# Cross-attention of layer 1: 256 keys of two batches per PSUM bank, the last key apart, and state-space preparation placed between tiles

## The chip, the cores and the metric

The kernel is one program on one core of one Trainium2 chip. The metric is device time in microseconds (us), the median of three runs. The core's engines each work through their own queue in order: TensorE (PE; its weight loads are PEld), VectorE (DVE), ScalarE (ACT), GpSimd (POOL), and SyncE (SP), which issues most DMAs. Matmuls write to PSUM, of which this program uses eight banks, 512 f32 values per partition each.

## The reference

The model takes `x`, 64 batches of 32 tokens with 256 channels, and a context of 257 keys per batch. Two layers each add three blocks to `x`, every one behind a normalisation:

```python
x = x + L0_xattn(ln(x), ctx, ctx, mask)    # softmax attention over 257 keys
x = x + L0_attn(ln(x))                     # a WKV recurrence and a channel mix
x = x + L0_ffn(ln(x))                      # mixture of 8 experts, the best 2
x = x + L1_xattn(ln(x), ctx)               # the change is here
x = x + L1_attn(ln(x))                     # selective state space, 16 states
x = x + L1_ffn(ln(x))                      # 8 experts of width 512
```

`L1_xattn` is grouped-query attention whose four projections are quantised: activations are divided by their root mean square, scaled to integers up to 127 by their largest magnitude, and multiplied with weights rounded to -1, 0, 1:

```python
xn = x * rsqrt(mean(x**2) + 1e-6)
scale = 127 / max(max(abs(xn)), 1e-5)
xq = clip(round(xn * scale), -128, 127) / scale
q, k, v = xq @ wq, ctxq @ wk, ctxq @ wv    # 16 heads of q, 8 of k and v, 16 wide
out = softmax(q @ k.T / 4) @ v             # 32 queries, 257 keys, per batch and head
out = ln(out) * gamma + beta               # then quantised and projected by wo
```

## The kernel before

The 2048 tokens are 16 tiles of 128 tokens (four batches each) in four blocks of 512. Each of the six sublayers is a stage, a function that returns one for a block: stages 0 to 2 are layer 0, stage 3 is the attention above, stage 4 the state space, stage 5 the feed-forward layer. `layers` (line 1140 on) calls them in a written order. The framework then puts every engine's instructions into an order of its own, in which work of different stages is mixed; the calls' order is the preference, buffers and data decide what can go.

**Stage 3** (`block`, line 693, and `tile3`, line 741). A block is normalised, each row is quantised (two roots in a row: `rstd`, then `rr`), and four tiles follow. `_rsqrt` computes a root by three refinement steps, of four GpSimd instructions each. For one tile, `tile3` loads the quantised context `cq` and the key scales `kb`, projects and transposes the queries, and spreads them into `qm`, where each of two key heads per quarter has its own rows. Then, for every one of four batches `e`:

- `keys(e)`: the projection of all 257 keys into one bank (line 787), times the scales (789). Values are projected for two batches at once (799) and copied by ScalarE (804).
- For each of four groups `h` of 32 rows: a score matmul over 257 keys into a bank (811), its maximum by VectorE (812), the exponential with its sum by ScalarE (813).
- The keys of the next batch.
- A transpose of the last key's weights (`pl`, 816), its copy (818), then two banks of four transposes of 128 keys each (824) with scaled copies (826).
- The weighted sum `oT_ps`: first the last key (831), by a matrix `vl` prepared per tile, then eight 32-column matmuls (835); two instructions take it to `od` (839, 840).

At the tile's end the sums are inverted and spread (`rs`, `rsm`, `rt`, lines 843 to 857), `od` is transposed (861) and scaled into `o4` (862). After four tiles the block is normalised, quantised again, projected by `wo` and added to `x` (lines 709 to 739). All PSUM tiles of stage 3 come from one pool `ps` of two banks.

**Stage 4.** `ahead(b)` normalises block b, projects it (918), convolves (936 to 943), and computes the step sizes `dt` (946 to 974), through a pool `psp` of one bank. `recur(b, v)` is the recurrence: for 16 states and two halves, GpSimd forms `g` (993), ScalarE an exponential (997), VectorE a scan (998) and a product (999), GpSimd adds (1000). It begins with `dtx` (981) and closes with the gate `zs` (1005), the output projection (1015) and a normalisation. The scans use a pool `psh` of two banks.

**Stage 5.** Each block passes 128 large matmuls (`up`, 1112, and `acc`, 1120), with pools of one and two banks.

The calls of interest:

```python
v = ahead(0)
s3(1)
s2(2)
later = ahead(1)
recur(0, v)
s2(3)
...
for b in range(1, NBLK):
    v = later
    if b + 1 < NBLK:
        s3(b + 1)
        later = ahead(b + 1)
    recur(b, v)
    s5(b - 1)
```

Of the kernel before, what the change touches and what calls it, by code (L numbers as in the profile page):

```python
# [8 lines left out]
F32 = mybir.dt.float32  # L9
# [6 lines left out]
P = 128  # L16
# [307 lines left out]
def _steps(k, am, rr, sc, dq):  # L324


    nc = k.nc
    nc.vector.tensor_tensor(am, am, rr, ALU.mult)
    nc.vector.tensor_scalar(am, am, 1e-5, None, ALU.max)
    nc.vector.tensor_scalar(dq, am, 1.0 / 127.0, None, ALU.mult)  # L330
    nc.vector.reciprocal(sc, am)
    nc.vector.tensor_scalar(sc, sc, 127.0, None, ALU.mult)
    nc.vector.tensor_tensor(sc, sc, rr, ALU.mult)


def _quant_rows(k, src, rr, ints, dq):

    nc = k.nc
    am = k.small.tile([P, 4], F32, name="am", tag="q_am")
    nc.vector.tensor_reduce(am, src, AX.X, ALU.max, apply_absolute_value=True)  # L340
    sc = k.small.tile([P, 4], F32, name="qsc", tag="q_sc")
    _steps(k, am, rr, sc, dq)
    for t in range(4):
        nc.vector.tensor_scalar(src[:, t, :], src[:, t, :], sc[:, t : t + 1], MAGIC, ALU.mult, ALU.add)
    nc.vector.tensor_scalar(ints, src, MAGIC, 127.0, ALU.subtract, ALU.min)
# [202 lines left out]
def _stage2(k, pool):  # L548
# [16 lines left out]
    def block(b):  # L565
# [32 lines left out]
        gt = wk.tile([P, 4, E, E], F32, name="gt", tag="gt", bufs=1)  # L598
        eq = wk.tile([P, 4, E, E], F32, name="eq", tag="eq", bufs=1)
# [14 lines left out]
        gT = wk.tile([E, BT], F32, name="gT", tag="gT", bufs=1)  # L614
# [49 lines left out]
def _stage3(k, w, tmp):  # L664

    nc, i = k.nc, k.i
# [12 lines left out]
    nc.vector.tensor_reduce(lgm, k.ident.rearrange("p (l n g) -> p l g n", l=2, g=2), AX.X, ALU.add)  # L679

    diag = w.tile([4, 4, 32], F32, name="diag", tag="diag")
    nc.vector.tensor_copy(diag, k.ident[0:4, 0:4].unsqueeze(2).to_broadcast([4, 4, 32]))
    pick = w.tile([4, 4, 4], F32, name="pick", tag="pick")
    nc.vector.tensor_copy(pick, k.ident[0:4, 0:4].unsqueeze(2).to_broadcast([4, 4, 4]))
# [3 lines left out]
    nc.vector.tensor_scalar(qsc, qsc, 0.25, None, ALU.mult)  # L688

    def ps(shape, name, dt=F32):  # L690
        return k.ps.tile(shape, dt, name=name, tag="s")

    def block(b):
        xs = [k.x[b][:, j, :] for j in range(4)]

        mv, rstd = _stats(k, xs, "3")
        xn = k.wk3.tile([P, 4, D], F32, name="xn3", tag="xn3", bufs=1)
        for j in range(4):
            _norm(k, xn[:, j, :], xs[j], mv, rstd, j)
        rr = k.small.tile([P, 4], F32, name="rr", tag="q_rr")  # L700
        nc.vector.tensor_tensor(rr, rstd, rstd, ALU.mult)
        nc.vector.tensor_tensor(rr, rr, mv[:, :, 1], ALU.mult)
        _rsqrt(k, rr, [(rr, 1.0, RMS_EPS)], "3r")
        xq = k.wk3.tile([P, 4, D], BF16, name="xq", tag="xq", bufs=1)
        dq = k.small.tile([P, 4], F32, name="dq", tag="dq")
        _quant_rows(k, xn, rr, xq, dq)
        nc.vector.tensor_scalar(dq, dq, qsc, None, ALU.mult)
        o4 = k.wk3.tile([P, 4, 4, 2, 2, 16], F32, name="o4", tag="xn3", bufs=1)
        for j in range(4):
            tile3(b, j, xq, dq, o4)  # L710
# [9 lines left out]
        ss = k.small.tile([P, 4], F32, name="ss", tag="q_ss")  # L720
        for j in range(4):
            junk = k.wk3.tile([P, D], BF16, name="junk", tag="junk", bufs=1)
            nc.scalar.activation(junk, y[:, j, :], AF.Square, accum_out=ss[:, j : j + 1])
        rr = k.small.tile([P, 4], F32, name="rr", tag="q_rr")
        _rsqrt(k, rr, [(ss, 1.0 / D, RMS_EPS)], "3r")
        yq = k.wk3.tile([P, 4, D], BF16, name="yq", tag="xq", bufs=1)
        dy = k.small.tile([P, 4], F32, name="dy", tag="dq")
        _quant_rows(k, y, rr, yq, dy)
        nc.vector.tensor_scalar(dy, dy, mw[:, 3:4], None, ALU.mult)
        for j in range(4):  # L730
# [8 lines left out]
            nc.vector.scalar_tensor_tensor(xs[j], wo_ps, dy[:, j : j + 1], xs[j], ALU.mult, ALU.add)  # L739

    def tile3(b, j, xq, dq, o4):
        g = 4 * b + j
# [13 lines left out]
        q = k.wk3.tile([P, D], F32, name="q", tag="q", bufs=1)  # L756
        nc.vector.tensor_scalar(q, q_ps, dq[:, j : j + 1], None, ALU.mult)
        qT_ps = ps([P, 2, 4, T], "qT_ps")
# [6 lines left out]


        vr_ps = ps([4, P], "vr_ps")
        for c in range(2):
            nc.tensor.matmul(vr_ps, cq[:, c, :, 2 * P], wkv[:, c, P : 2 * P], start=c == 0, stop=c == 1)
        vr = k.wk3.tile([4, P], F32, name="vr", tag="vr", bufs=1)  # L770
        nc.scalar.activation(vr, vr_ps, AF.Copy, scale=k.dql[:, g : g + 1])
        vl_ps = ps([4, 4, P], "vl_ps")
        for e in range(4):
            nc.tensor.matmul(vl_ps[:, e, :], pick[:, e, :], vr, start=True, stop=True)
        vl = k.wk3.tile([4, 4, P], F32, name="vl", tag="vl", bufs=1)
        nc.vector.tensor_tensor(vl, vl_ps, diag.rearrange("i j c -> i (j c)").unsqueeze(1).to_broadcast([4, 4, P]), ALU.mult)


# [94 lines left out]
def _stage4(k, w, wk):  # L873
# [35 lines left out]
    def pp(shape, name):  # L909
        return k.psp.tile(shape, F32, name=name, tag="p")  # L910
# [367 lines left out]
```

## Time and profile before

| what | value |
|---|---|
| runs before (three) | 2100.08, 2110.91, 2112.42 us; median 2110.91 |
| the profiled execution | 2109.35 us, span 2107.4 us |
| mean granted TensorE clock | 0.822 of full speed |
| PE / DVE / ACT / POOL busy | 80 / 61 / 47 / 48% of the span |
| DMA | 149.96 MB, mean 71 GB/s |

A row of the page's groups names the line, engine and operation, the tile written and those read, shapes and count; then busy time, the mean of one in ns, and the idle time just before them with what ended most of it. TensorE's f32 matmuls show as two records each. The clock is that which the chip granted TensorE, as a share of full speed. Where the text cuts the span into stretches, the times are those at which named instructions start or end in the trace.

### The profile page before, as it was taken

To read this page: it belongs to the slowest core of one execution; us is meant where nothing else is said; L and a number is where in the kernel's file an instruction comes from. 1 tells how busy PE (TensorE), PEld (TensorE's weight loads), DVE (VectorE), ACT (ScalarE), POOL (GpSimd) and SP (SyncE) were. 2 spreads that over 40 slices of the span, in tenths; PEclk is the share of its full clock that TensorE was granted. 3 is DMA by queue.
4 is the path that set the end of the run, shared out by engine and by line. 5 is a ranking of instruction groups with operands and counts; after the bars stand their busy time and mean duration, and the time that the engine had idled before them with its cause. 6 is when DMAs were issued, how large, how long until landed. Compare 5 with 4: busy or idle time off the path is not lost. (4 is left out here: it accounts for less than half of the span.)

```text
span 2107.4 us, 20682 instructions
## 1 busy us (share of the span) xinstructions
PE 1696.1 (80%) x6647; PEld 837.2 (40%) x6647; DVE 1288.8 (61%) x2472; ACT 988.0 (47%) x2060; POOL 1014.2 (48%) x1069
## 2 busy tenths in 40 slices
PE   4768967768979969877878799988899958874598
PEld 2334534334545533444434344434344533322243
DVE  4587594675483466898567886344888433776200
ACT  3444352302545326555235577436777616662132
POOL 4444445313130224777527787122889332998200
PEclk8677976868978979655685899988999969996799
DMA  7654232210000101221012132111233002331021
GB/s 235 220 175 147 86 126 81 72 41 0 21 21 20 58 1 52 61 63 63 6 32 80 48 121 72 42 59 52 76 114 100 21 20 63 111 118 40 11 80 40
DMA packets 87543, 149.96 MB, mean 71 GB/s; under 512 B 7673, under 2 KB 51979, under 8 KB 85387
## 3 DMA queue, kind: packets, MB, share of 16 engines
q1 hardware_dynamic: 84868, 147.69, 22.9%
q10 hardware_dynamic: 2566, 0.96, 0.2%
q8 instruction: 52, 0.85, 0.2%
q14 instruction: 57, 0.46, 0.1%
HBM read 137.71 MB, written 10.91 MB: 71 GB/s over the span
## 5 line engine op out<-in xcount | busy, mean ns | idle before, releaser
L998 DVE TENSOR_TENSOR_SCAN h<-h,g 128x512 f32<-128x512 f32 x256 | 306.2, 1218 | 62.8 <-ACT h L997 42.6
L993 POOL TENSOR_TENSOR g<-dtx,bc 128x1024 f32<-128x1024 f32 x128 | 300.3, 2352 | 82.3 <-DVE h L998 37.7
L1000 POOL TENSOR_TENSOR xc<-xc,hc 128x1024 f32<-128x1024 f32 x128 | 301.0, 2355 | 32.9 <-DVE hc L999 31.0
L1112 PE MATMUL up<-xT,w 128*128 128x512 f32 x512 | 274.1, 648 | 18.1 <-ACT hid L1114 17.6
L1120 PE MATMUL acc<-hid,w 128*128 128x512 f32 x512 | 261.3, 627 | 28.5 <-ACT hid L1116 28.5
L997 ACT ACTIVATE h<-dt,A 128x512 f32<-128x512 f32 x256 | 173.2, 688 | 100.1 <-DVE hc L999 98.1
L811 PE MATMUL sc<-kT,qm 32*128 32x257 f32 x512 | 179.6, 514 | 29.1 <-ACT p L813 13.7
L813 ACT ACTIVATE p<-sc,nm 128x257 f32<-128x257 f32 x256 | 119.9, 471 | 133.5 <-DVE nm L812 131.8
L999 DVE TENSOR_TENSOR hc<-h,bc 128x512 f32<-128x512 f32 x256 | 170.3, 679 | 3.3 <-POOL xc L1000 1.1
L812 DVE TENSOR_REDUCE nm<-sc 128x1 f32<-128x257 f32 x256 | 102.8, 416 | 110.3 <-PE sc L811 108.6
L89 POOL TENSOR_TENSOR rs_t<-rs_r 128x4 f32<-128x4 f32 (+3 forms) x150 | 33.4, 227 | 267.8 <-DVE rs_r L87 236.9
L625 PE MATMUL weps<-we,xT 128*128 128x512 f32 x256 | 145.5, 693 | 12.3 <-DVE x L621 6.5
L1120 PEld LDWEIGHTS acc<-hid,w 128*128 128x128 f32 x512 | 94.1, 197 | 140.1 <-issue 92.2
L1112 PEld LDWEIGHTS up<-xT,w 128*128 128x128 f32 x512 | 93.6, 201 | 130.1 <-issue 81.5
L1114 ACT ACTIVATE hid<-up,chan 128x512 f32<-128x512 f32 x128 | 87.0, 680 | 113.0 <-PE up L1112 112.6
L811 PEld LDWEIGHTS sc<-kT,qm 32*128 32x128 f32 x512 | 80.3, 220 | 138.1 <-ACT p L813 54.0
L230 POOL TENSOR_TENSOR cT<-cT,scb 128x2056 f32<-128x2056 f32 x16 | 74.8, 4678 | 55.9 <-DMA scb<-scales 45.9
L824 PE MATMUL pt_ps<-ident,p 128*128 128x128 f32 x512 | 89.6, 320 | 9.9 <-DVE kT L789 8.2
L826 ACT ACTIVATE pt<-pt_ps,cdq 128x512 f32<-128x512 f32 x128 | 84.0, 680 | 27.9 <-PE pt_ps L824 27.8
L525 POOL TENSOR_TENSOR kk<-kk 128x512 f32<-128x512 f32 x32 | 33.1, 1040 | 126.6 <-ACT kk L524 126.6
L824 PEld LDWEIGHTS pt_ps<-ident,p 128*128 128x128 f32 x512 | 71.7, 165 | 40.4 <-DVE kT L789 15.9
L918 PE MATMUL inps<-xT,w_L_attn_in_projT 128*128 128x512 f32 x128 | 68.7, 664 | 22.5 <-DVE hc L999 21.9
(385 smaller groups left out, 3070.1 us busy)
## 6 DMA issues: line engine op xcount, KB each, us to landing
bc<-rows SPq DMA_DIRECT2D x64, 512.0 KB
w<-in_L_ffn_w_dram SPq DMA_DIRECT2D x64, 512.0 KB
cT<-in_ctxT_dram SPq DMA_DIRECT2D x16, 1028.0 KB
cq<-cq SPq DMA_DIRECT2D x32, 514.0 KB
cn<-in_ctx_dram SPq DMA_DIRECT2D x64, 256.0 KB
scb<-scales SPq DMA_DIRECT2D x16, 514.0 KB
kb<-steps SPq DMA_DIRECT2D x16, 514.0 KB
x<-in_x_dram SPq DMA_DIRECT2D x4, 512.0 KB
```

Source lines behind the costliest of these rows:

```text
L625: nc.tensor.matmul(ps, xT[:, c, r], we[:, c, e : e + 2, :], start=c == 0, stop=c == 1)
L811: nc.tensor.matmul(sc, qm[r, e].rearrange("p l n g -> p (l n g)"), kT[r, :], start=True, stop=True)
L812: nc.vector.tensor_reduce(nm[:, h : h + 1], sc, AX.X, ALU.max, negate=True)
L813: nc.scalar.activation(p[:, h, :], sc, AF.Exp, bias=nm[:, h : h + 1], accum_out=sm[:, e, h : h + 1])
L824: nc.tensor.transpose(pt_ps[:, h, :], p[:, h, m * P : (m + 1) * P], k.ident)
L993: nc.gpsimd.tensor_tensor(g, dtx[:, c2 : c2 + 2], bc[:, 0:1, :].to_broadcast([P, 2, BT]), ALU.mult)
L997: nc.scalar.activation(h, dt, AF.Exp, scale=A[:, c2 + c, n : n + 1])
L998: nc.vector.tensor_tensor_scan(h, h, g[:, c, :], 0.0, ALU.mult, ALU.add)
L999: nc.vector.tensor_tensor(hc[:, c, :], h, bc[:, 1, :], ALU.mult)
L1000: nc.gpsimd.tensor_tensor(y[:, c2 : c2 + 2], y[:, c2 : c2 + 2], hc, ALU.add)
L1112: nc.tensor.matmul(u, w1[e][:, c, q * P : (q + 1) * P], xT[:, c, :], start=c == 0, stop=c == 1)
L1120: nc.tensor.matmul(acc[o], w2[e][:, q, o * P : (o + 1) * P], hid[e][:, q, :], start=n == H, stop=n == E * H + H - 1)
```

## The change

It has five parts.

1. *Keys, scores, sums.* `tile3` becomes `attend`, which returns four steps. `keys(e)` projects 256 keys of two batches into one bank, and the values of both, which VectorE scales on the way out. `scores(e, h0)` computes two groups of two batches: two banks, each with the 256 scores of both; one maximum instruction per bank, one minimum against the last key's negated score, four exponentials. `sums(e)` transposes and sums as before, without the last key.
2. *The last key.* Its key, value and score are computed once per tile (`last_ps`, `sl_ps`, `nsl`). `back()` adds its weight to the sums and its share to the output, through one matmul with `each` and one GpSimd addition.
3. *Emission.* A block is a loop of nine half-overlapped steps: scores of the next pair of batches stand ahead of the sums of the one before.
4. *Quantisation.* `_quant_rows` works on the centred or unscaled rows, and the root enters only the scale that is applied later (`dq`, `dy`).
5. *Banks and order.* The single bank of `psp` becomes `psx`; stage 3 and `ahead` share three banks, one of three allocations going to `psx` once it is open. `ahead(b)` is split into `norm`, `convolve` and `step`, which `s3(b + 1)` calls after its first three tiles. Layer 0's expert stage keeps `gt`, `eq` and `gT` in one shared buffer.

```diff
-def _quant_rows(k, src, rr, ints, dq):
+def _quant_rows(k, src, floor, ints, am):
...
+def _bank(k, shape, name, dt=F32):
+    k.turn += 1
+    return (k.psx if k.psx and k.turn % 3 == 0 else k.ps).tile(shape, dt, name=name, tag="s")
...
-        for j in range(4):
-            tile3(b, j, xq, dq, o4)
+        tiles = {}
+        for u in range(9):
+            j, e = divmod(2 * u, 4)
+            if u < 8:
+                if e == 0:
+                    tiles[j] = attend(4 * b + j, j, xq, dq, o4)
+                tiles[j].keys(e)
+                tiles[j].scores(e, 0)
+            if u:
+                last, le = tiles[(u - 1) // 2], (2 * u - 2) % 4
+                last.sums(le)
+                last.sums(le + 1)
+            if u < 8:
+                tiles[j].scores(e, 2)
+            if u and le == 2:
+                last.back()
+                if between:
+                    between.pop(0)()
...
+        def scores(e, h0):
+            hs = range(h0, h0 + 2)
+            sc = {h: ps([P, 2, 2 * P], "sc") for h in hs}
+            for f in range(2):
+                for h in hs:
+                    r = slice(32 * h, 32 * h + 32)
+                    nc.tensor.matmul(
+                        sc[h][:, f, :], qm[r, e + f].rearrange("p l n g -> p (l n g)"), kTs[e][r, f, :],
+                        start=True, stop=True,
+                    )
+            for h in hs:
+                nc.vector.tensor_reduce(nm[:, e : e + 2, h], sc[h], AX.X, ALU.max, negate=True)
+            n2 = nm[:, e : e + 2, h0 : h0 + 2]
+            nc.vector.tensor_tensor(n2, n2, nsl[:, e : e + 2, h0 : h0 + 2], ALU.min)
+            w_ = ws[e, h0 // 2] = k.wk3.tile([P, 2, 2, 2 * P], F32, name="p", tag="p", bufs=3)
+            for h in hs:
+                for f in range(2):
+                    nc.scalar.activation(
+                        w_[:, f, h - h0, :], sc[h][:, f, :], AF.Exp, bias=nm[:, e + f, h : h + 1],
+                        accum_out=sm[:, e + f, h : h + 1],
+                    )
...
+        def back():
...
+            nc.vector.tensor_tensor(pl, nm, nsl, ALU.subtract)
+            nc.scalar.activation(pl, pl, AF.Exp)
+            nc.vector.tensor_tensor(sm, sm, pl, ALU.add)
...
+            t = k.wk3.tile([P, 2, 8, 16], F32, name="ol", tag="q_ol", bufs=1)
+            nc.vector.tensor_tensor(t, vl_ps.unsqueeze(1).to_broadcast([P, 2, 8, 16]), over(1), ALU.mult)
+            nc.gpsimd.tensor_tensor(o, o, t, ALU.add)
...
-        k.psh, k.psp, k.psu = pool("psh", 2, **psum), pool("psp", 1, **psum), pool("psu", 1, **psum)
+        k.psh, k.psx, k.psu = pool("psh", 2, **psum), pool("psx", 1, **psum), pool("psu", 1, **psum)
...
             s2(1)
-            v = ahead(0)
+            parts, v = ahead(0)
+            for part in parts:
+                part()
+            s2(2)
             s3(1)
-            s2(2)
-            later = ahead(1)
             recur(0, v)
             s2(3)
...
         for b in range(1, NBLK):
-            v = later
+            parts, v = ahead(b)
             if b + 1 < NBLK:
-                s3(b + 1)
-                later = ahead(b + 1)
+                s3(b + 1, parts)
+            else:
+                for part in parts:
+                    part()
             recur(b, v)
             s5(b - 1)
```

## The prediction

> **What bounds the kernel now.** I read the page first, then cut the span at the four recurrences of the state space, because they are the only stretches in which GpSimd is nearly full. The page's totals name no single bound:
>
> ```profile
> span 2107.4 us, 20682 instructions
> PE 1696.1 (80%) x6647; PEld 837.2 (40%) x6647; DVE 1288.8 (61%) x2472; ACT 988.0 (47%) x2060; POOL 1014.2 (48%) x1069
> ```
>
> A recurrence runs from its `dtx` (line 981; starts at 811, 1109, 1460, 1778 us) to its last addition to `xc` (line 1000; ends at 1020, 1305, 1643, 1936 us). I call them R0 to R3. The view of busy time by stretch, cut there (columns: stretch and length, busy us of each engine with instructions, granted TensorE clock, DMA share, GB/s):
>
> ```profile
> 811.00:1020.00 209.00, 168.80 (x775) 90.26 (x774) 181.00 (x300) 111.82 (x269) 156.16 (x78) 0.58 0.20 56
> 1020.00:1109.00 89.00, 70.05 (x180) 31.99 (x180) 54.49 (x154) 24.98 (x39) 35.99 (x90) 0.82 0.06 19
> 1109.00:1305.00 196.00, 172.37 (x728) 83.98 (x728) 163.48 (x255) 128.54 (x256) 158.44 (x92) 0.84 0.29 86
> 1305.00:1460.00 155.00, 138.66 (x589) 67.12 (x587) 65.45 (x196) 78.13 (x156) 34.59 (x100) 0.89 0.14 42
> 1460.00:1643.00 183.00, 170.03 (x728) 75.06 (x728) 152.25 (x227) 137.68 (x260) 155.09 (x69) 0.97 0.32 93
> 1643.00:1778.00 135.00, 105.38 (x386) 51.38 (x385) 45.94 (x137) 63.29 (x107) 29.10 (x87) 0.84 0.12 36
> 1778.00:1936.00 158.00, 103.77 (x214) 40.32 (x213) 119.17 (x136) 89.44 (x114) 154.99 (x71) 0.85 0.33 93
> 1936.00:2107.00 171.00, 138.51 (x342) 64.67 (x340) 15.60 (x53) 43.86 (x49) 17.38 (x46) 0.89 0.13 40
> ```
>
> GpSimd works 155 to 158 us in each recurrence. Beside the feed-forward layer alone (R3) the recurrence takes 158 us: that is its floor. R0, R1 and R2 have attention tiles beside them and take 209, 196 and 183 us. Between them lie gaps of 89, 155 and 135 us in which GpSimd is mostly idle: the next recurrence waits for attention of its own block, then norm, projections, convolution and step size. So time is made of floors, stretching and gaps, and the gaps are set by how long an attention tile takes.
>
> Inside a tile the groups are these:
>
> ```profile
> L811 PE MATMUL sc<-kT,qm 32*128 32x257 f32 x512 | 179.6, 514 | 29.1 <-ACT p L813 13.7
> L813 ACT ACTIVATE p<-sc,nm 128x257 f32<-128x257 f32 x256 | 119.9, 471 | 133.5 <-DVE nm L812 131.8
> L812 DVE TENSOR_REDUCE nm<-sc 128x1 f32<-128x257 f32 x256 | 102.8, 416 | 110.3 <-PE sc L811 108.6
> ```
>
> Each engine idles about as long as it works and waits for the one before it: a chain score, maximum, exponential over two banks. The tile of scores in the last tile of block 2 (1318 to 1368 us, no recurrence beside it) says who ends whose wait:
>
> ```profile
> its engine sat idle before it (us, times) until:
>   DVE nm L812: 11.6, 9
>   PE sc L811: 8.2, 7
>   DVE od L840: 4.1, 3
> ```
>
> From `rsm` to `rsm` (line 846) a tile takes 45 us at its quickest (681 to 726, block 0), 59 us beside the feed-forward layer without a recurrence (1309 to 1368, 1622 to 1681), 55 to 73 us beside recurrences.
>
> **The change, part by part.** *Work.* TensorE loses the `pl` transposes (19.8 us in all), the `vl` matmuls (19.8) and the four-row matmul ahead of each sum (36.5), and gains a few narrow ones; about 60 us of record time, 4 us a tile. Score matmuls are ordered so that neighbours use different row groups. In this trace one score matmul (two records) occupies 0.69 us, and where two heads were issued together (1328.1 us) both took 0.70 us: they ran side by side. Four should then take about 0.43 + 0.70 = 1.13 us in place of about 1.75. ScalarE loses the `v` copy (18.6), the `pl` copy (16.0) and some of `pt` (680 ns with a scale, 581 ns as the plain copy of `v`: 128 x 0.1 = 13), gains 32 small ones at 0.25: about -40 us. VectorE: 256 maxima at 416 ns become 128 over twice the width, estimated 0.42 + 0.26 = 0.68 us (87 for 103); `kT` 64 x 0.41 becomes 32 x 0.68 (22 for 26); `v` comes here (32 x 0.68 = 22); `vl` goes (-11); minima, last key and the end of the tile add some 35: about +30 us, 2 us a tile. GpSimd gains 16 additions of 128x256, at 0.75 us by line 1023: 12 us. These sums move little in a kernel of 2107 us; the waits decide.
>
> *The chain of a tile.* With two banks and one head at a time I estimate for one batch: four heads at 2.0 us per bank trip (0.69 + 0.42 + 0.67 and handovers) over two banks, 4 us; then keys, last key, two transposes with 0.68 us evacuations and the sum, 3.5 to 4 us: 7.5 to 8 us, four times, plus 8 to 13 us between tiles: 40 to 45, which is the quickest tile seen. The same bookkeeping for two batches with three banks: scores 1.1, two maxima 1.3, minimum 0.2, four exponentials 2.7; twice; the transposes of the previous pair use the third bank meanwhile, and two sums (2.6 each) come between: 14 us per pair, 28 a tile. The order of the changed program puts the next tile's projection ahead of the previous tile's last sums, so I add 4 and not 8 to 13: 32 us uncontended, against 45. Beside the feed-forward layer the old tile took 59: 59 x 32/45 = 42, and I use 41.
>
> [...]
>
> *Order.* This is the largest part. The program's order shows the state-space preparation of block b handed out between tiles of attention b+1, and recurrence b behind them. Built that way, R1's step size stands behind the first half of attention 2's last tile, so R1 no longer runs beside attention 2, only beside the first tile of attention 3; R2 only beside the end of attention 3. Gap for gap, from the order and the rows:
> - Up to R0: one refinement of an inverse root leaves the end of block 0's attention (12 GpSimd rows of 0.2 us and handovers, about 5 us), two leave the front, where layer 0 covers them. Without the third bank (it is opened only afterwards) scores hold both banks: estimated 17.7 us per pair, 35 plus turnover, about the old 45. I take -5 (between -15 and +20): R0 starts at 806.
> - R0: VectorE is 87% busy there. Its instructions from the end of layer 0 to R0's end sum to 266 us before and 267 after by the rows' means. End unchanged: 1020.
> - First gap: what remains of R0's block (35 us: output projection, normalisation, projections), 3.5 tiles of attention 2 at 41, 8 us to `dtx`: 187 us, in place of 89. TensorE must pass some 140 us of matmuls at full clock in it: the tiles, about 70 of the 128 large ones of feed-forward block 0, and layer 0's last expert matmuls. [...] The rows show 0.58 in R0, where TensorE waits often, and 0.84 to 0.97 where it is dense. At 0.9 the 140 us need 156 and fit; at half clock they need 280. The gap will be dense, so I take 0.9.
> - R1: 158 floor, plus 13 for GpSimd's small rows and additions that come beside it: 171, in place of 196.
> - Second gap: 7 us, 3.4 tiles at 41, 8: 155, as before.
> - R2: 171, in place of 183.
> - Third gap: preparation of block 3 no longer waits for attention 3; norm, projection and convolution lie in R2. Left are the `zs` product and output projection (16 us in the rows from 1936), `ssm_ps` and `dt_ps` (7 us) and 14 us from there to `dtx` (1763.8 to 1777.6): 40, in place of 135.
> - R3 158, end 172 (three or four us of feed-forward block 2 may slip there).
>
> New waits: transposes of a sum wait for the bank of a score, and behind them in TensorE's queue stand feed-forward matmuls and the next keys; that is why 41 and not 32. The preparation's bank allocations join the rotation of three in place of owning one; they are 8 per block, each under 2 us, so between 0 and 15 us per block, taken at 0 since they stand in TensorE's idle time. The load of the key scales (one buffer) must wait until the second pair of keys; before it waited for the fourth key, later in the tile. On SyncE it is queued among the `bc` loads, which wait for VectorE; a tile beside R1 can be late, 0 to 10 us, taken at 0 because R1 doesn't wait for that tile. Layer 0's expert layer shares one buffer where it had three: 0 to 5 us under R0.
>
> Sum: 806 + 214 + 187 + 171 + 155 + 171 + 40 + 158 + 172 = 2074, against 2107. The profiled execution lies 2 us above its span (2109.35), and the median of three another 1.6 (2110.91): 2077.
>
> **The rivals.** *Serialisation costs more than the tile gains (slower).* The first and second gaps hold 6.9 tiles. Break-even is where 2074 + 6.9 x (T - 41) = 2107: a tile of 45.7 us. For it: a tile beside the feed-forward layer takes 59 now, in-order queues add to each link, and the clock may drop. Against: three banks, and the pairs. At 50 us a tile: 2136, median 2139.
> *The recurrences don't shrink (no change).* If R1 and R2 keep 196 and 183 because the stretching comes from ScalarE's table switches and feed-forward work, not from tiles: +37, 2114. R3 at 158 speaks against it.
> *The tile reaches its uncontended pace (faster).* At 33 us: 2019, median 2022. The order places the feed-forward matmuls where the tile waits; yet no tile of the old kernel got there.
> *The change doesn't do what it says*: score pairs don't overlap. Then 0.6 us per group of four, 16 groups in 4 tiles, 2.5 us a tile: 2091, inside the forecast's own range.
>
> **How the numbers follow.** Forecast 0.43 (own range 2050 to 2105), serialisation 0.30, recurrences kept 0.12, pace 0.15. About 1% is what a measurement of this kernel tells from no change. Faster by over 1% means under 2090: three quarters of the forecast and all of the last, 0.48. Slower, over 2132: most of the first rival and the upper ends of block 0's two banks and the doubled maximum, 0.32. The rest 0.20. The range is 2015 to 2150.
>
> **What would show it.** The recurrences' starts: R1 about 100 us later than before (1207), R3 about 35 us earlier (1744). Gaps near 187, 155, 40; R1 and R2 near 171. `rsm` to `rsm` near 41 us in the middle of blocks 2 and 3; groups of four score matmuls at 1.1 us; granted clock near 0.9 in the gaps. I am wrong if tiles there take over 46 us, if the third gap stays near 100, or if R0 ends well after 1020.

## The result and the profile after

The changed kernel takes 2179.92 us (median of four runs, 2174.85 to 2183.0), the kernel before 2107.11 (2100.08 to 2112.42) in the same comparison: 1.0345 times as long, with an interval of 1.0305 to 1.0386. The prediction was 2077, between 2015 and 2150: the time moved the other way, and beyond the range.

The page of the changed kernel opens with its span and the busy time of each engine:

```profile
span 2181.2 us, 20218 instructions
PE 1609.8 (74%) x6455; PEld 818.5 (38%) x6455; DVE 1360.9 (62%) x2444; ACT 927.9 (43%) x1990; POOL 1020.4 (47%) x1037
```

TensorE lost 86 us of work and ScalarE 60, VectorE gained 72, and the span grew by 74. No engine is fuller than before as a share of the span, except VectorE by one point. So the loss is one of overlap. The busy time by stretch, cut at the recurrences as before (`dtx`, line 1045, to the last addition to `xc`, line 1064), shows where:

```profile
0.00:760.00 760.00, 583.74 (x2595) 316.40 (x2596) 487.59 (x983) 289.66 (x780) 270.45 (x423) 0.83 0.28 92
760.00:1017.00 257.00, 178.57 (x838) 98.48 (x838) 223.40 (x364) 107.24 (x281) 169.09 (x109) 0.63 0.18 48
1017.00:1223.00 206.00, 191.69 (x923) 99.44 (x922) 98.14 (x257) 99.69 (x230) 27.53 (x77) 0.93 0.18 55
1223.00:1426.00 203.00, 97.87 (x313) 44.47 (x312) 165.95 (x221) 86.46 (x152) 166.25 (x106) 0.68 0.22 65
1426.00:1597.00 171.00, 153.36 (x777) 82.79 (x776) 66.80 (x175) 89.20 (x205) 22.82 (x53) 0.90 0.12 38
1597.00:1793.00 196.00, 100.84 (x299) 42.52 (x298) 158.93 (x203) 98.01 (x151) 170.85 (x106) 0.75 0.24 65
1793.00:1841.00 48.00, 34.78 (x104) 19.58 (x104) 15.80 (x46) 11.49 (x15) 18.07 (x39) 0.78 0.08 23
1841.00:2003.00 162.00, 120.02 (x248) 45.60 (x247) 125.12 (x143) 100.22 (x126) 154.84 (x78) 0.94 0.34 94
2003.00:2181.00 178.00, 148.97 (x368) 69.23 (x366) 19.19 (x61) 45.96 (x53) 20.51 (x50) 0.90 0.14 44
```

Before, TensorE worked 172 of the 196 us of R1 and 170 of the 183 of R2. Now it works 98 of 203 and 101 of 196, and the gap ahead of R1 has TensorE busy in 192 of its 206 us while GpSimd does 28. What ran side by side now runs in turn: TensorE's part in the gap, GpSimd's and VectorE's part in the recurrence. The longest of TensorE's waits in R2 is a single one (view of waits, 1597 to 1793 us; total, times, longest):

```profile
PE inps L975 <- DVE hc L1063: 58.5, 1, 58.5
```

From 1731.5 to 1789.9 us the next work in TensorE's order is the projection for the gate `zs` of R2 itself, which takes a bank of the scans' pool, and it is released only by a late `hc` of that recurrence. In the kernel before, TensorE is never idle for more than 12 us in R0, R1 or R2.

Stage by stage, in us (start to R0, R0, gap, R1, gap, R2, gap, R3, end), rounded:

| kernel | start | R0 | gap | R1 | gap | R2 | gap | R3 | end |
|---|---|---|---|---|---|---|---|---|---|
| before | 811 | 209 | 89 | 196 | 155 | 183 | 135 | 158 | 171 |
| predicted | 806 | 214 | 187 | 171 | 155 | 171 | 40 | 158 | 172 |
| after | 760 | 257 | 206 | 203 | 171 | 196 | 48 | 162 | 178 |

The groups inside a tile, from the view of groups by line:

```profile
L840 PE MATMUL sc<-kT,qm 32*128 32x256 f32 x512 | 124.3, 488 | 32.2 <-ACT p L851 19.8 <-DVE kT L821 6.1 <-DVE od L879 2.1
L851 ACT ACTIVATE p<-sc,nm 128x256 f32<-128x256 f32 x256 | 117.8, 473 | 80.8 <-DVE nm L847 72.6 <-DVE rs_v L84 8.0
L845 DVE TENSOR_REDUCE nm<-sc 128x2 f32<-128x512 f32 x128 | 85.1, 686 | 39.6 <-PE sc L840 37.9
L847 DVE TENSOR_TENSOR nm<-nm,nsl 128x4 f32<-128x4 f32 x64 | 20.4, 318 | 1.7
```

The chain inside a tile did get shorter: VectorE's wait for scores fell from 109 to 38 us, ScalarE's for a maximum (now the minimum behind it) from 132 to 73. The doubled maximum takes 686 ns (680 was estimated). The last row is new: the minimum has four columns per row, and its mean of 318 ns hides two kinds, as shown below. In the tile of block 2 from 1192 to 1242 us (R1 starts 31 us into it) hardly anything waits for scores; the first two rows of the view that the prediction shows for the old tile:

```profile
its engine sat idle before it (us, times) until:
  PE sc L840: 1.3, 3
  issue: 0.8, 3
```

That tile still takes 50 us from `rsm` to `rsm`, because TensorE is nearly full in it (45.5 us busy): feed-forward matmuls stand between its steps.

### The profile page after: what moved, and what is told of

It is laid out like the page before. It is cut to its first block, busy times and chain, and to the rows that moved or that the text cites. A ratio compares the mean times of both kernels' runs of the same rounds, so it can differ in the third digit from the quotient of the medians.

```text
span 2181.2 us, 20218 instructions
## 1 busy us (share of the span) xinstructions
PE 1609.8 (74%) x6455; PEld 818.5 (38%) x6455; DVE 1360.9 (62%) x2444; ACT 927.9 (43%) x1990; POOL 1020.4 (47%) x1037
## 5 line engine op out<-in xcount | busy, mean ns | idle before, releaser
L1062 DVE TENSOR_TENSOR_SCAN h<-h,g 128x512 f32<-128x512 f32 x256 | 302.9, 1215 | 45.5 <-POOL g L1057 31.2
L1184 PE MATMUL acc<-hid,w 128*128 128x512 f32 x512 | 251.7, 615 | 21.2 <-ACT hid L1180 21.2
L851 ACT ACTIVATE p<-sc,nm 128x256 f32<-128x256 f32 x256 | 117.8, 473 | 80.8 <-DVE nm L847 72.6
L840 PE MATMUL sc<-kT,qm 32*128 32x256 f32 x512 | 124.3, 488 | 32.2 <-ACT p L851 19.8
L620 PE MATMUL weps<-we,xT 128*128 128x512 f32 x256 | 134.3, 658 | 11.2 <-DVE x L622 7.8
L919 POOL TENSOR_TENSOR o<-o,ol 128x256 f32<-128x256 f32 x16 | 11.7, 729 | 235.7 <-DVE ol L918 233.9
L864 PE MATMUL pt_ps<-ident,p 128*128 128x128 f32 x512 | 96.4, 325 | 23.7 <-DVE pp L451 8.3
L845 DVE TENSOR_REDUCE nm<-sc 128x2 f32<-128x512 f32 x128 | 85.1, 686 | 39.6 <-PE sc L840 37.9
L866 ACT COPY pt<-pt_ps 128x512 f32<-128x512 f32 x128 | 72.8, 588 | 68.1 <-PE pt_ps L864 65.6
L879 DVE SCALAR_TENSOR_TENSOR od<-oT_ps,half,od 128x64 f32<-128x64 f32 x64 | 17.6, 276 | 132.6 <-ACT od L878 132.6
L840 PEld LDWEIGHTS sc<-kT,qm 32*128 32x128 f32 x512 | 72.4, 226 | 73.3 <-ACT p L851 21.9
```

The source lines that it names most:

```text
L620: nc.tensor.matmul(ps, xT[:, c, r], we[:, c, e : e + 2, :], start=c == 0, stop=c == 1)
L840: nc.tensor.matmul(sc[h][:, f, :], qm[r, e + f].rearrange("p l n g -> p (l n g)"), kTs[e][r, f, :], start=True, stop=True,)
L851: nc.scalar.activation(w_[:, f, h - h0, :], sc[h][:, f, :], AF.Exp, bias=nm[:, e + f, h : h + 1], accum_out=sm[:, e + f, h : h + 1],)
L864: nc.tensor.transpose(pt_ps[:, h, m, :], ws[e0, hp][:, f, h, m * P : (m + 1) * P], k.ident)
L1062: nc.vector.tensor_tensor_scan(h, h, g[:, c, :], 0.0, ALU.mult, ALU.add)
L1184: nc.tensor.matmul(acc[o], w2[e][:, q, o * P : (o + 1) * P], hid[e][:, q, :], start=n == H, stop=n == E * H + H - 1)
```

## The experiments

The kernel before had medians of 2105 to 2109 us beside these runs; ratios are to it.

**Which part loses?** The theory O was the prediction's own: the order of calls decides. The rivals were the shared third bank and the order of the scores.

*Old call order.* The changed kernel, with the preparation of a block called in one piece (`whole`) behind the attention tiles of that block, and attention 1 again ahead of layer 0's expert block 2:

```diff
...
-            parts, v = ahead(b)
+            v = later
             if b + 1 < NBLK:
-                s3(b + 1, parts)
...
+                s3(b + 1)
+                later = whole(b + 1)
```

> The changed attention with its three shared banks, but the calls in the order of the kernel before: preparation of block b+1 whole, right behind attention b+1, and attention 1 ahead of layer 0's expert block 2. Theory O (the order of the calls is what costs: recurrences lost their cover): faster than before, 2030 to 2070 us, with the first recurrence starting about 40 us earlier than in the kernel before and the gaps between recurrences back near 89, 155 and 135 us or below. Theory A (the new attention itself costs: two banks of scores held through four exponentials, VectorE's added work): 2140 us or more, near the changed kernel's 2180.

Measured: 2152.32 us, ratio 1.0209 (1.0161 to 1.0257). Stages 762, 270, 23, 278, 38, 227, 128, 173, 249. Theory O is refuted: the old order takes 28 us off, not the 110 or more that it forecast, and the kernel stays slow. R1 takes 278 us, and 444 of the 1024 feed-forward records are left after R3 (256 before), which is the long end.

*Order alone.* The attention, banks and quantisation of before, with the parts of `ahead(b)` handed out between tiles of attention b+1:

```diff
...
-                s3(b + 1)
-                later = ahead(b + 1)
+                s3(b + 1, parts)
...
```

> The attention, quantisation and banks of the kernel before, with the changed order of the calls alone: preparation in three parts between the tiles of the next attention, recurrence behind it. Theory O: slower than the changed kernel, 2230 to 2290 us, since the tiles in the two gaps take 59 and not 49 us (6.9 x 10 = 69) and the first recurrence starts later. Theory A: 2090 to 2130 us.

Measured: 2096.13 us, 0.995 (0.9931 to 0.9969). Stages 808, 203, 138, 176, 141, 185, 122, 156, 174. The order by itself gains 10 us. R1 starts at 1150 us, not at 1223: the framework took the preparation's instructions ahead of where they are called (`ssm_ps` of block 1 begins at 1124 us, before the first tile of attention 2 ends at 1139). That their free bank is what let it is tested below.

*An own bank for the preparation.* The changed kernel, attention on its two banks, the preparation alone on the third:

```diff
-    return (k.psx if k.psx and k.turn % 3 == 0 else k.ps).tile(shape, dt, name=name, tag="s")
+    return k.ps.tile(shape, dt, name=name, tag="s")
...
-        return _bank(k, shape, name)
+        return k.psx.tile(shape, F32, name=name, tag="s")
```

> The changed kernel, but attention keeps two banks and the preparation has the third one for itself. If the third bank is what makes the new tiles faster, tiles in the middle of blocks 2 and 3 take 55 to 58 us in place of 49 and the kernel 2215 to 2240 us. If it does nothing, 2170 to 2190 us.

Measured: 2098.05 us, 0.9958 (0.9938 to 0.9978): 82 us faster than the changed kernel and below both expectations, although attention has one bank less. Its tiles are slower (55 to 76 us in blocks 2 and 3, against 44 to 52). Against the changed kernel R0 is 26 us shorter and the first two gaps 64 and 69 (142 and 102 in place of 206 and 171); R1, R2 and the third gap take back 16, 22 and 39. R1 and R2 run beside attention again:

```profile
1139.00:1358.00 219.00, 179.99 (x724) 83.62 (x723) 173.68 (x250) 137.08 (x259) 165.04 (x96) 0.89 0.29 80
1460.00:1678.00 218.00, 178.45 (x779) 84.49 (x778) 170.85 (x229) 136.54 (x268) 155.49 (x69) 0.91 0.27 75
```

TensorE is busy 180 us in R1 here, 98 in the changed kernel.

*Scores head by head.* The changed kernel, with the two batches as the inner loop, so that neighbouring score matmuls use the same row group:

```diff
-            for f in range(2):
-                for h in hs:
+            for h in hs:
+                for f in range(2):
```

> The changed kernel with its score matmuls ordered head by head, so that neighbours share a row group. If alternating row groups saves 0.6 us per group of four, groups take about 1.7 in place of 1.1 us and the kernel 10 to 40 us more (2190 to 2220 us). If neighbours did not overlap or the time is hidden, 2170 to 2190 us.

Measured: 2159.74 us, 1.0242 (1.0203 to 1.028), 20 us faster than the changed kernel, where slower was expected. What that means is taken up below.

**Is it the sharing?** Theory S: by taking banks in turn with attention, the preparation is tied to the place where it is called, behind the tiles.

*Own bank and head by head.*

> The changed kernel with attention on its two banks, the preparation alone on the third, and scores emitted head by head. The own bank alone gave 2098 us, the head order alone took 20 us off the changed kernel. If the two causes are separate (sharing of the bank; the alternating order of row groups): 2075 to 2085 us. If the head order only helped because it kept the shared bank busy for less time: no more than the own bank alone, 2092 to 2104.

Measured: 2096.34 us, 0.9956 (0.9934 to 0.9979). The 20 us of the head order are not there when the preparation has its own bank.

*New attention, old order, own bank.* The own-bank edit and the old-order edit together.

> The new attention and quantisation with two banks for attention, the third for the preparation alone, and the calls in the order of the kernel before (preparation of a block in one piece, after the attention tiles of the block). Theory S (the shared bank is the loss, the call order is nearly neutral): 2090 to 2115 us. Theory O (the new call order costs): under 2070. If the new attention needs the new order to pay: over 2125, the second and third gap over 150 us each.

Measured: 2100.42 us, 0.9968 (0.995 to 0.9985). With an own bank, the call order is worth 2 us, which is within the noise. Stages 769, 250, 67, 231, 124, 221, 108, 160, 172.

*Old attention, shared bank.* The order-alone kernel, with its attention and its preparation both on `_bank`:

```diff
     def ps(shape, name, dt=F32):
-        return k.ps.tile(shape, dt, name=name, tag="s")
+        return _bank(k, shape, name, dt)
     def pp(shape, name):
-        return k.psp.tile(shape, F32, name=name, tag="p")
+        return _bank(k, shape, name)
```

> The attention of the kernel before, the new call order, and the three banks taken in turn by attention and preparation. With an own bank for the preparation this was 2096 us. Theory S: sharing by itself ties the preparation to the tiles whatever the attention inside them: over 2130 us, the second recurrence starts after 1180 us (1150 with the own bank). If sharing only hurts together with the new attention's pairs (three scores' banks held at once): 2085 to 2110.

Measured: 2247.65 us, 1.0667 (1.0631 to 1.0704). Sharing costs the old attention 151 us. Stages 801, 229, 233, 194, 176, 202, 12, 181, 220. Two rows of its view by stretch repeat the picture of the changed kernel (gap ahead of R1, then R1):

```profile
1031.00:1263.00 232.00, 211.09 (x951) 104.25 (x952) 98.70 (x282) 106.49 (x226) 31.54 (x110) 0.92 0.13 42
1263.00:1457.00 194.00, 101.67 (x350) 43.77 (x348) 160.11 (x229) 93.60 (x170) 165.23 (x104) 0.71 0.26 71
```

*Three banks for attention alone.* The changed kernel, with the preparation on the two banks of the recurrence:

```diff
     def pp(shape, name):
-        return _bank(k, shape, name)
+        return ph(shape, name)
```

> The changed kernel with all three banks in turn for attention alone; the preparation takes its banks from the two of the recurrence. Theory S (preparation behind tiles' banks): attention keeps its tile of about 49 us, and the preparation is freed: R1 starts before 1200, total 2090 to 2140. If the third bank in the attention is itself what crowds the recurrences (VectorE full): about as the changed kernel, 2160 to 2200. If the preparation on the recurrence's two banks waits for the recurrence before it: over 2200, the gaps over 200.

Measured: 2085.93 us, 0.9889 (0.9838 to 0.994), a little under theory S's range. One line of the kernel changed, 94 us gained. Attention keeps its third bank and its tile of about 50 us; only the partner in the rotation is gone. What it moves is seen when block 1's preparation runs. Times in us from the traces:

```
kernel                      ssm_ps of block 1   dtx of R1
before                      1090                1109
order alone, own bank       1124                1150
old attention, shared       1246                1263
changed, shared             1207                1223
changed, own bank           1108                1139
changed, three + ph         1099                1124
```

In the changed kernel `ssm_ps` begins after the third tile's `rsm` (1192 us), where it is called. With separate banks it runs before the first (1104), with the same calls. Theory S holds for both attentions in the new call order. All pairs of runs that differ in the sharing, in us:

| attention | calls | shared | separate | cost of sharing |
|---|---|---|---|---|
| new | new | 2180 | 2098 own bank, 2086 three + ph | 82, 94 |
| new, no minimum (below) | new | 2137 | 2049 three + ph | 88 |
| new, head by head | new | 2160 | 2096 own bank, 2098 three + ph (below) | 63, 62 |
| old | new | 2248 | 2096 own bank, 2092 three + ph (below) | 151, 155 |
| new | old | 2152 | 2100 own bank | 52 |

The last pair does not fit theory S as stated: with the old calls `ssm_ps` of block 1 runs no later with the shared bank (1032 against 1067 us), and the loss shows as feed-forward work left behind R3 (444 records against 256). How sharing leads to that stays open. A second sign goes with the sharing: an idle time of TensorE of over 17 us inside R2 or R3 is found only in kernels with the new calls and a shared bank (58 us in the changed kernel, 18 head by head, 28 without the minimum, 36 and 58 with the old attention), apart from one of 22 in R3 of the two kernels with the old attention, old quantisation and an own bank.

**What do the other parts give?**

*Three banks and head by head.*

> Three banks for attention alone, the preparation on the recurrence's banks, and scores emitted head by head. Theory S1 (head order helps only where a score's bank is wanted by the preparation too): 2078 to 2092 us, as with row groups in turn (2086). Theory S2 (row groups in turn are slower by themselves, by the 20 us seen in the changed kernel): 2060 to 2072.

Measured: 2097.58 us, 0.9967 (0.9952 to 0.9983): 12 us slower than row groups in turn, above either forecast. With the shared bank the head order gained 20, with an own bank 2. So the order of row groups has no effect of its own that these runs can show; it shifts the arrangement. The traces of the changed kernel and of its head-by-head variant fit that: 20 of the 64 groups of four score matmuls take 1.13 us with row groups in turn, and 22 take 1.14 us head by head, where 1.7 was expected.

*No minimum.* Three banks for attention, without the minimum of maxima and last key (the exponent is taken against the maximum of 256 keys, which leaves the softmax the same):

```diff
-            n2 = nm[:, e : e + 2, h0 : h0 + 2]
-            nc.vector.tensor_tensor(n2, n2, nsl[:, e : e + 2, h0 : h0 + 2], ALU.min)
```

> Three banks for attention alone, the preparation on the recurrence's banks, and the minimum over the 256 keys and the last key left out (64 small VectorE instructions; the exponent is taken against the maximum of 256 keys alone, which a softmax allows). In the trace of that kernel 17 of these minima that began beside a long GpSimd instruction took 1.05 us instead of 0.16, and held the exponentials behind them. Theory P (VectorE instructions with both inputs in SBUF stand still beside GpSimd, and that stretches the recurrences): 2060 to 2076 us, the recurrences R0 to R2 together at least 15 us shorter than 254, 236, 222. If VectorE is simply full there: 64 x 0.16 = 10 us less work at most, 2078 to 2088.

Measured: 2049.32 us, 0.9741 (0.9707 to 0.9775): 37 us for 64 instructions of 0.16, more than either theory gave; R0, R1 and R2 are 28 us shorter together (252, 222, 210). It is the fastest kernel of this study, level with one below.

*Old attention, three banks.*

> The attention of the kernel before, the new call order, three banks in turn for attention alone, the preparation on the recurrence's banks. With two banks and an own bank for the preparation: 2096 us; with the bank shared: 2248. If the gain of the same edit on the new attention (2098 to 2086) is the third bank's: 2078 to 2090. If only attention in pairs can use the third bank: 2092 to 2104. If the loss in the shared case was not the preparation's waiting but the rotation itself (banks taken in a fixed turn): over 2150.

Measured: 2092.22 us, 0.9931 (0.9914 to 0.9949): the third bank is worth 4 us to the old attention at most (the intervals overlap), and rotation is harmless as long as it stays within attention.

*Quantisation alone.* The kernel before with only `_quant_rows` and its callers changed.

> The kernel before with the quantisation of the changed one alone (inverse root after the maximum instead of before it). In the changed kernel the first recurrence starts 46 us earlier than before. If the quantisation is what pulls block 0's attention forward: the last tile of block 0 ends before 715 (726 before), R0 starts before 795, total 2085 to 2103. If the start is owed to the attention tiles (end of layer 0's keys seven us earlier, tiles in pairs): rsm at 720 to 728, R0 at 805 to 812, 2100 to 2112.

Measured: 2059.9 us, 0.9791 (0.975 to 0.9831). Stages 774, 219, 73, 199, 150, 182, 129, 157, 172. The first quantised rows of block 0 are written at 489 us instead of 514, the last tile of block 0 ends at 687 instead of 726, and R0 starts 37 us earlier. The whole early start of the changed kernel (760), except 14 us, is this part.

**Do the parts add, and why does the minimum cost so much?**

*Shared bank, no minimum.*

> The changed kernel, bank shared, with only the minimum over 256 keys and last key left out. If the two losses add (82 for sharing, 37 for the minimum): 2136 to 2150 us. If in the shared case the preparation's place is all that decides: 2170 to 2185. If a shorter tile also moves the preparation forward: under 2130.

Measured: 2137.02 us, 1.0164 (1.0126 to 1.0203): 43 us less than the changed kernel. Here the losses by bank and by minimum add; a run below shows that this is no rule.

*Minimum aside.* Three banks for attention; the minimum stays in its place, into a tile `low` that nobody reads:

```diff
-            nc.vector.tensor_tensor(n2, n2, nsl[:, e : e + 2, h0 : h0 + 2], ALU.min)
+            low = k.small.tile([P, 2, 2], F32, name="low", tag="low")
+            nc.vector.tensor_tensor(low, n2, nsl[:, e : e + 2, h0 : h0 + 2], ALU.min)
```

> Three banks for attention alone, the preparation on the recurrence's banks (2086 us with the minimum, 2049 without); here the minimum is computed where it was, but into a tile that nobody reads, and the exponent is taken against the maximum of 256 keys. Theory C (the exponentials' wait for the minimum is the cost): 2045 to 2058. Theory P (the instruction on VectorE's queue is the cost, standing beside GpSimd): 2075 to 2092.

Measured: 2084.16 us (2072.18 to 2094.93), 0.9895 (0.9845 to 0.9946). The exponentials no longer wait for the minimum, and nearly the whole cost stays. So the exponentials' wait for the minimum is not what costs.

*Minimum aside, one input from PSUM.*

```diff
-            nc.vector.tensor_tensor(low, n2, nsl[:, e : e + 2, h0 : h0 + 2], ALU.min)
+            nc.vector.tensor_tensor(low, n2, sc[h0][:, :, 0:2], ALU.min)
```

> As the run with the minimum into a tile that nobody reads (2084 us; 2049 without any minimum), but its second input is taken from the scores in PSUM, so only one input lies in SBUF; the exponent is taken against the maximum of 256 keys. Theory P (two SBUF inputs stand still beside GpSimd): none of the 64 takes over 0.4 us, and the time is 2050 to 2066. If any further instruction between maximum and exponential costs as much: 2076 to 2092.

Measured: 2073.86 us (2068.19 to 2091.84), 0.9844 (0.9808 to 0.9881), between the two expectations. The instruction itself behaved as theory P says. These rows are VectorE's groups in the same stretch (1111 to 1250 us) of the two kernels, first with two inputs in SBUF:

```profile
L848 DVE TENSOR_TENSOR low<-nm,nsl 128x4 f32<-128x4 f32 x9 | 8.2, 909 | 0.0
```

and with one of them in PSUM:

```profile
L848 DVE TENSOR_TENSOR low<-nm,sc 128x4 f32<-128x4 f32 x11 | 1.6, 149 | 0.0
```

Over the whole kernel 15 of 64 took 0.4 to 2.1 us with both in SBUF, and none over 0.16 with one in PSUM. VectorE's total fell from 1359 to 1349 us. Whether the time followed is not shown: the medians are 2084 and 2074, but their intervals overlap. From 2074 to the 2049 without a minimum 25 us stay. Two things are in these 25 and were not separated: 10 us of VectorE's own work (64 x 0.15), and whatever the framework orders differently.

*Parts together, old attention: three banks.*

> The attention of the kernel before with the quantisation of the changed one, the new call order, three banks for attention, the preparation on the recurrence's banks. If the quantisation's 46 us add to the 13 of order and banks: 2042 to 2052 us. If they gain at the same place: 2055 to 2065, no better than the quantisation alone.

Measured: 2068.53 us, 0.9819 (0.9792 to 0.9847): above both expectations, and no better than the quantisation alone.

*Parts together, old attention: own bank.* The order-alone kernel with the quantisation added.

> The attention of the kernel before, the quantisation and the call order of the changed one, two banks for attention and one for the preparation alone. Quantisation alone gave 2060 us, the order alone 10 us: if they add, 2044 to 2056; if not, 2056 to 2072, as with three banks for attention (2069).

Measured: 2051.93 us, 0.9734 (0.9704 to 0.9765). Quantisation and order add (46 and 10).

*New attention in the old order, own bank, no minimum.*

> The changed attention and quantisation in the old call order, two banks for attention and one for the preparation, without the minimum (with it 2100 us; quantisation alone with the old attention 2060). If the minimum is all that the new attention loses: 2055 to 2068. If the pairs gain by themselves: under 2050. If two heads' and two batches' scores in two banks lose as well: over 2075.

Measured: 2149.77 us, 1.0206 (1.0179 to 1.0232): 49 us slower than the same kernel with the minimum, which none of the expectations had. R3 starts 12 us earlier (1758 against 1770), but 380 feed-forward records instead of 256 are left after it, and the last stretch takes 221 us:

```profile
1929.00:2150.00 221.00, 196.25 (x481) 90.14 (x479) 19.05 (x60) 66.18 (x73) 20.31 (x50) 0.94 0.17 55
```

Fewer attention instructions left the feed-forward layer behind. Why the framework put it later was not found. The run bounds what can be claimed of any edit here: leaving out the same 64 instructions gave -43, -37 and +49 us in three arrangements, through the order that is built.

## Why the prediction was wrong, step by step

Two questions have different answers here: what made the kernel slow, and which terms of the prediction's sum were off.

*What made it slow.* The runs form a chain in which each kernel adds one part to the one ahead of it: before 2106; quantisation 2060 (-46); call order 2052 (-8); new attention with an own bank for the preparation 2098 (+46); the shared bank 2180 (+82). The prediction priced the last two of these wrongly.

*Which terms were off.* The sum was 2074 and the span is 2181, 107 us more: R1 and R2 57 of them (203 and 196 for 171 and 171), the first two gaps 35 (206 and 171 for 187 and 155), the third gap, R3 and the end 18. The start was 46 us too late and R0 43 too short, which cancel.

- **Banks: the failed step.** "The preparation's bank allocations join the rotation of three in place of owning one; they are 8 per block, each under 2 us, so between 0 and 15 us per block, taken at 0". The time that a bank is held was priced, not the place in the turn. It costs 82 us, and 151 with the old attention. Before, the preparation ran early in its own bank; once it takes its turn with the tiles, in the new order of calls, it runs where it is called.
- **Order.** The prediction saw the preparation's late place and put it down to the calls. The place was right (R1 was to start at 1207, it starts at 1223), its cause was not: the same calls with separate banks start R1 at 1111 to 1150. And the late place was to be paid back by short recurrences and a short third gap. The third gap did come (48, predicted 40). The short recurrences did not, and that is the second failed step.
- **R1 and R2: 171 predicted, 203 and 196 measured.** The rival that recurrences don't shrink named the size, not the reason: ScalarE's table loads took 1.28 us each, 8 of them in R1 and 11 in R2 (10 and 14 us), against 11 and 15 before (14 and 19). Two things go with their length. First, R1 to 1294 us runs beside the end of attention 2 (output projection at 1283, normalisation): it starts its ninth step of 32 after 69 us, R2 after 71, R3 after 49. Second, VectorE is nearly full after that (91 to 96% in R1, 90 and then 100% in R2), and GpSimd with it (86 to 98%): the other 24 steps take 134 and 126 us, in R3 113. The trace of 1737 to 1793 us, in R2, shows VectorE's groups without a gap:

```profile
L1062 DVE TENSOR_TENSOR_SCAN h<-h,g 128x512 f32<-128x512 f32 x21 | 24.5, 1208 | 0.0
L1003 DVE SCALAR_TENSOR_TENSOR xc<-xpad,chan,xc 128x512 f32<-128x512 f32 x10 | 17.7, 1774 | 0.0
```

  Before, the same convolution of block 3 ran in the gap (1739 to 1752 us), with GpSimd idle:

```profile
L943 DVE SCALAR_TENSOR_TENSOR xc<-xpad,chan,xc 128x512 f32<-128x512 f32 x12 | 9.0, 752 | 10.1 <-ACT xc L939 9.8
```

  Moved beside GpSimd, each takes 1774 ns instead of 752. The prediction added 13 us for what comes beside R1 and R2, and took VectorE's durations from rows with an idle GpSimd. To size this, I took the VectorE instructions that overlap a GpSimd instruction of over 1.5 us and subtracted the median of the same group elsewhere: in R0, R1 and R2 the excess was 15, 13 and 7 us before, 32, 25 and 21 after, together 43 us more of VectorE's time. That is not the same as lost time: by the same reckoning the fastest kernel (no minimum, 2049 us) has about 73 us in these three. How much of the 32 and 25 us that R1 and R2 missed by is owed to each of the two was not tried apart.
- **Gaps: 187 and 155 predicted, 206 and 171 measured.** "140 us of matmuls ... at 0.9 ... 156 and fit": the clock was 0.93, but TensorE had 192 us of records in the first gap (`up` and `acc` 76, expert matmuls 20, the rest attention and state space), by estimate 178 at full clock (192 x 0.93). The 280 at half clock rested on no gap: the three were granted 0.82 to 0.89 before and 0.78 to 0.93 after. A granted 0.50 stands in the last 56 us of R2, with TensorE busy 3 of them. Nor does the clock simply follow how dense TensorE is: before, R0 had 0.58 with TensorE busy 81% of it, R3 0.85 with 66%. The tile of 41 became 44 to 52, with TensorE busy 47 of 48 us and 45 of 50 in the last two of attention 2. (Of the two old tiles that the 59 us rest on, the one from 1622 us had R2 beside it until 1643.) Against the break-even of 45.7 this says slower, as the main rival did, whose price of 2139 is still 41 short, since it kept R1 and R2 at 171.
- **Score groups.** The 1.13 us were right where they were meant: 20 of the 64 groups take just that, 19 of them in the first two gaps. The mean of busy time, 1.94 (124.3 / 64), mixes in slower groups, among them those with records of about 629 ns in place of 374 (111 of 512, 87 of these in R0, R1 and R2, where the clock was 0.63 to 0.75). The waits between score, maximum and exponential fell nevertheless.
- **New attention.** Taken as a gain of the tile alone. With order, banks and quantisation the same, it costs 46 us (2052 to 2098; the step holds two smaller parts too, which no run has apart: layer 0's shared expert buffer, and `xn4` in the preparation's ring of three buffers): R0, R1 and R2 take 231, 219 and 218 us in place of 207, 174 and 179, while the start and the gaps give back 68 (16, 4, 37 and 11). The excess beside GpSimd is 70 us in these three, against 19 with the old attention. Many of its small instructions have both inputs in SBUF. The 46 hold for this arrangement: in the old order with an own bank it is 40 (2060 to 2100), with three banks 17 (2069 to 2086), and with three banks and no minimum the new attention gains 19 (2069 to 2049).
- **Quantisation.** "Two leave the front, where layer 0 covers them ... I take -5". It is -46, the largest gain of any part: R0 starts at 774 instead of 811 with it alone. Layer 0 did not cover it. In the changed kernel nothing of it survives R0, which starts at 760 and still ends at 1017; with the quantisation alone R0 ends at 994.
- **What held.** The third gap, R3 (158, 162), the end (172, 178), the maxima (680, 686 ns), the plain `pt` copy (581, 588), GpSimd's addition (750, 729). R0's end came out at 1017, predicted 1020, by luck: its start was 46 us early and R0 43 longer. The rows were right; the overlap was not. The doubled maximum was not tried apart: no run shows the loss that the chance of slower counts for it, only 686 ns where two of 416 ns stood before.

## What to carry to other kernels

A buffer pool is part of the order: two stages that take banks in turn from one rotation are coupled at each allocation, and the early work of one can be held to the late work of the other. Before pooling buffers, ask which of the two runs ahead today, and because of which free buffer; here the lead that was lost cost more than the time a bank is held (52 to 155 us in the pairs above). When work moves beside another engine, take its duration from rows that ran there, and split a change into parts, since here a gain of 54 us lay hidden under a loss of 128.

## What the hardware showed

In these traces VectorE instructions with their inputs in SBUF could take longer beside long GpSimd instructions. The convolution step went from a mean of 752 ns (before, 1739 to 1752 us) to 1774 (after, 1737 to 1793 us), a 128x256 scaling of `xn` (line 333, one tensor input) from 345 (after, 440 to 520 us) to 1175 (after, 1294 to 1376 us), and the four-column minimum, in the run that puts it aside, from 0.16 to as much as 2.1 us, which is near the 2.38 us of one GpSimd instruction of the recurrence. It can be more than one: in R1 of the changed kernel one minimum took 5.75 us and ended with the third of three GpSimd instructions that followed each other without a gap (start and length in us, from the timeline):

```profile
1386.84 5.75 DVE L847 TENSOR_TENSOR nm<-nm,nsl 128x4 f32<-128x4 f32 x1
1385.61 4.66 POOL L1064 TENSOR_TENSOR xc<-xc,hc 128x1024 f32<-128x1024 f32 x2
1390.22 2.34 POOL L1057 TENSOR_TENSOR g<-dtx,bc 128x1024 f32<-128x1024 f32 x1
```

The waiting instruction of VectorE did not get its turn between two of GpSimd's. With one input in PSUM (the run with the minimum aside and one input from there) the minimum never took over 0.16 us, and the scans and the products behind them, which have one as well, never took over 1.24 and 0.70 us in the traces before and after. The rows show the wait; what in the chip causes it, no trace here shows. What it is worth in the kernel's time was not shown: with the minimum free of it the median was 2074 us, with the wait 2084, and the intervals overlap.
